# A decoder layer on one core: the steps that quantize the feed-forward's weights are spread over two batches instead of three

## The chip, the cores and the metric

The kernel runs on one core of a Trainium2 chip. The core has a matrix engine (TensorE; in the profile PE, with its weight loads as PEld), a vector engine (VectorE, DVE), an activation engine (ScalarE, ACT), a general engine (GpSimd, POOL) and SyncE (SP), which here only issues transfers. Sixteen DMA engines move data between the chip's main memory and the core's memories. Each engine works through its own queue in order; an instruction that waits holds up whatever is queued behind it on the same engine. The metric is device time in microseconds (us), the median of the runs; lower is better.

## The reference, cut to what matters

The kernel computes one decoder layer in float32 for a batch of four sequences of 512 rows of 512 numbers:

```python
x = x + attn(layernorm(x))                 # 16 heads over 128 x 128, all of a sequence's rows in q, k and v
x = x + gamma * xattn(layernorm(x), ctx)   # 8 heads, softmax over 512 keys
x = x + ffn(layernorm(x))

def ternary_quant(w):
    s = mean(abs(w))
    return clip(round(w / s), -1, 1) * s

def ffn(x):
    g = silu(x @ ternary_quant(w1).T) * (x @ ternary_quant(w3).T)
    return g @ ternary_quant(w2).T
```

w1 and w3 are 1365 x 512, w2 is 512 x 1365. A weight's scale s is a mean over the whole matrix, so quantizing takes two passes: one over all of it for the sum of absolute values, and one that compares each number with half the mean. The kernel keeps only the signs (-1, 0, 1), and applies s to the products.

## The kernel before, in words

**Stages.** The first batch's attention comes first (in the profile up to about 207 us). It loads the attention's weights, and keeps prepared copies of them (high parts, low parts and differences: `kept_kh`, `kept_kl`, `kept_kd` and so on) in main memory. Then a loop over b = 1, 2, 3 (line 989) does the attention of the second, third and fourth batch, about 216 us each. Within a batch a loop over j takes the four groups of heads. Each group makes three products, with the weights o (`values_out`, tiles `pu`), k (`keys_of`, `py`) and v (`values_of`, `pm`), and then the scores with q. A group's weights are 40 tiles of 256 KB, 12 each for o, k and v and 4 for q. They are loaded by SP (line 196) into a ring of 18 buffers (`wp`), so a load waits until an earlier tile's last matmul is done. At the end (from 858 us) all four batches go through the feed-forward.

**Work beside the products.** Two streams of small steps are woven between the products. Both are generators, and a class `Side` (line 165) advances them: after `done` calls of `tick()` out of `of`, it has taken `n * done / of` steps, rounded up. `products` (line 343) calls `tick` six times, so a batch has `TICKS` = 4 x 3 x 6 = 72 ticks.

- `side` is the cross-attention of the batch before (`cross`, line 694; tiles `xs`, `xp`, `xo`), after the row norms that it needs (`row_norms`). Its loads (`xd`, `kd`, `keys`, `xc`) and the store `x_c` are issued by POOL (line 703).
- `quant` is the quantizing of w1, w3 and w2, in this order (`quantize_steps`, line 621), 73 steps in all. w1 and w3 are cut into 12 pieces each, w2 into 11, of up to 128 x 512. A summing step takes a piece (`abs_w...`), and DVE sums its absolute values. After the last piece of a matrix, one step adds the sums up over the partitions (a matmul with one column) and makes the scales. A ternary step takes a piece again (`tern_w...`), DVE makes the signs (lines 652 and 653), and POOL stores them to main memory (`t_w...`, line 660).

**Loads of the pieces.** `staged` (line 595) issues them on POOL into a ring of three buffers, `stp`; `ahead` (line 612) issues a piece's load one step before the piece is used. A load into a buffer waits for what last used that buffer: DVE's sum of the piece before, or the landing of that piece's store.

**Order.** A planner orders each engine's queue when the kernel is built. It may bring an instruction forward when nothing that it needs is missing. The kernel therefore ties steps to a point in time by data: `settle` (line 606) multiplies a piece's first column by a one that DVE makes from `recent`, the latest product's tile (`one_of`, line 601). So DVE can't begin a piece before the product beside which the step stands. The loads into the staging buffers have no such tie. `tc.issue_after` puts some instructions behind another of their engine by name.

**Around it.** In the second batch (b = 1) DVE also makes difference tiles that the first batch did not keep (`od`, `kd`, `vd`, line 336), and POOL stores them. At the start of each batch POOL stores the attention's result (`x_a`), loads the next accumulators (`acc`) and adds the bias to them (line 872), and sends the row norms through main memory (`norm_a`, `norms`). At the end of the fourth batch SP loads the quantized weights (`t`, from 808 us on); the stores of w2 come last before that.

Of the kernel before, what the change touches and what calls it, by code (L numbers as in the profile page):

```python
# [20 lines left out]
B, T, D = 4, 512, 512  # L21
# [18 lines left out]
def decoder_layer_kernel(  # L40
# [124 lines left out]
    class Side:  # L165
# [5 lines left out]
        def tick(self):  # L171
            self.done += 1
            while self.n and self.n * self.done > self.of * self.taken:
                self.taken += 1
                next(self.steps, None)
# [249 lines left out]
    def parts_of(b, xs):  # L425
        tris = []
        for g in range(NG):
            tri = Tri(*(x3p.tile([P, D], F32R, tag="x3", name=f"x{p}_{b}_{g}") for p in "hld"))
            tri_of(tri, xs[g])
            tris.append(tri)  # L430
        return tris
# [4 lines left out]
    def gram_upper(b, xs, midway=None):  # L436
        pool, tag = (x3p, "x3") if b == 0 else (yp, "y")
        G = [pool.tile([P, D], F32, tag=tag, name=f"G_{b}_{m}") for m in range(KC)]
        pg = {}

        def add(m, g):
            if g == 0:
                pg[m] = bank(f"pg_{b}_{m}")
            nc.tensor.matmul(  # L444
                pg[m][:, : D - m * P],
                lhsT=xs[g][:, ts(m, P)],
                rhs=xs[g][:, m * P :],
                start=(g == 0),
                stop=(g == NG - 1),
            )  # L450
            if g == NG - 1:
                evict(G[m][:, m * P :], pg[m][:, : D - m * P])


        if b == 0:
            order = [(m, g) for g in range(NG) for m in range(KC)]
        else:
            order = [(m, g) for m in range(KC) for g in range(NG)]
        for m, g in order:
            add(m, g)  # L460
            if midway and (m, g) == (1, NG - 1):
                midway()
        return G

    def gram_rest(b, G):

        for rows in ((1, 2), (3,)):
            pt = bank(f"gt_{b}_{rows[0]}")
            n = 0
            for j in rows:  # L470
                for i in range(j):
                    nc.tensor.transpose(pt[:, ts(n + i, P)], G[i][:, ts(j, P)], ident)
                evict(G[j][:, : j * P], pt[:, n * P : (n + j) * P])
                n += j
        tris = []
        for m in range(KC):
            tri = Tri(*(g3p.tile([P, D], F32R, name=f"g{p}_{m}") for p in "hld"))
            tri_of(tri, G[m])
            tris.append(tri)
        return tris  # L480
# [73 lines left out]
    def turned(b, j, e):  # L554
        eT = ep.tile([P, NG, DH], F32, tag="eT", name=f"eT_{b}_{j}")
        transpose_blocks(eT, e, f"pe_{b}_{j}", True)
        return eT

    def output(b, j, eT, ms, accs):
        for g in range(NG):  # L560
            po = bank(f"po_{b}_{j}_{g}")
            nc.tensor.matmul(po, lhsT=eT[:, g, :], rhs=ms[g], start=True, stop=True)  # L562
            scale = (S if exact("o", b, j) else 1.0) * (S if exact("v", b, j) else 1.0)
            nc.vector.scalar_tensor_tensor(accs[g], po, scale, accs[g], ALU.mult, ALU.add)
            if j == HG - 1:
                nc.gpsimd.dma_start(by_group(x_a[b], g), accs[g])
# [54 lines left out]
    def quantize_steps(name):  # L621

        pieces = pieces_of(name)
        sums = small.tile([P, len(pieces)], F32, tag=f"sums_{name}", bufs=1, name=f"sums_{name}")
        nc.vector.memset(sums, 0.0)
        for piece, t, i in ahead(pieces, f"abs_{name}"):
            nc.vector.tensor_reduce(  # L630
                sums[: piece.shape[0], i : i + 1],
                piece,
                AX.X,
                ALU.add,
                apply_absolute_value=True,
            )
            yield
        col = small.tile([P, 1], F32, tag="col", name=f"col_{name}")
        nc.vector.reduce_sum(col, sums, axis=AX.X)
        tot = bank(f"tot_{name}")  # L640
        nc.tensor.matmul(tot[:, 0:1], lhsT=ones, rhs=col, start=True, stop=True)

        s = scales[name]
        for i, f in enumerate((0.5, -0.5, -1.0)):
            nc.vector.tensor_scalar(
                s[:, i : i + 1], tot[:, 0:1], 1.0 / (HID * D), f, ALU.mult, ALU.mult
            )
        yield
        for piece, t, i in ahead(pieces, f"tern_{name}"):
            r, n = piece.shape  # L650
            above = stp.tile([P, 512], BF16, tag="above", bufs=1, name=f"above_{name}_{i}")
            nc.vector.tensor_scalar(above[:r, :n], piece, s[:r, 0:1], None, ALU.is_gt)
            nc.vector.scalar_tensor_tensor(
                piece, piece, s[:r, 1:2], above[:r, :n], ALU.is_lt, ALU.subtract
            )
            for columns, place in t:
                part = piece[:, columns]
                if len(place.shape) > 2:
                    part = part.rearrange("p (u c) -> p u c", c=P)
                nc.gpsimd.dma_start(place, part)  # L660
            yield

    def quantize():
        for name in ("w1", "w3", "w2"):
            yield from quantize_steps(name)

    QUANTIZE_STEPS = 2 * (6 * KC + NHC) + 3
# [7 lines left out]
    def row_norms(b, accs):  # L675


        mv = small.tile([P, NG, 2], F32, tag="mvc", bufs=2, name=f"mv_c_{b}")
        for g in range(NG):
            yield  # L680
            yield
            moments(mv[:, g, :], accs[g], f"c_{b}_{g}")
        rstd = rstd_of(mv, f"c_{b}")
        mean, var = (mv[:, :, i : i + 1].rearrange("p c s -> p (c s)") for i in range(2))
        nc.vector.tensor_scalar(mean, mean, -1.0, None, ALU.mult)
        nc.vector.tensor_copy(var, rstd)
        nc.gpsimd.dma_start(norm_a[b].rearrange("(p g) s -> p g s", g=NG), mv)
        norms[b] = small.tile([P, 2 * NC, 2], F32, tag="norms", bufs=2, name=f"norms_{b}")
        for half in (slice(0, XD), slice(XD, P)):
            nc.gpsimd.dma_start(norms[b][half], norm_a[b].rearrange("(n p) s -> p n s", p=XD))  # L690
        for _ in range(3):
            yield
# [142 lines left out]
    TICKS = HG * 3 * 6  # L835
# [20 lines left out]
    def bias_rows(b):  # L856
        t = yp.tile([P, D], F32, tag="y", name=f"bo_bc_{b}")
        (nc.gpsimd if b > 0 else nc.sync).dma_start(t, bo.to_broadcast([P, D]))
        return t
# [21 lines left out]
    for j in range(HG):  # L881
# [19 lines left out]
        def midway():  # L901
            if waiting:
                waiting[2] = turned(*waiting[:3])
# [72 lines left out]
        inputs_f[b] = halves  # L976


    quant = Side(quantize(), QUANTIZE_STEPS, (B - 1) * TICKS)
    cpool = [  # L980
        cpools.enter_context(tc.tile_pool(name=n, bufs=k, side="right"))
        for n, k in (("c_x", 1), ("c_in", 2), ("c_p", 4), ("c_pt", 2))
# [6 lines left out]
    for b in range(1, B):  # L989
        def midway():  # L990
            waiting[2] = turned(*waiting[:3])

        G = gram_upper(b, xs, midway)
        recent[:] = [G[0], G[0]]
        output(*waiting)
        side = Side(
            itertools.chain(row_norms(b - 1, waiting[4]), cross(b - 1, *cpool)),
            NORM_STEPS + CROSS_STEPS,
            TICKS + 6,
        )  # L1000

        def tick():
            quant.tick()
            side.tick()

        bo_bc = bias_rows(b)
        g3 = gram_rest(b, G)
        for j in range(HG):
            u3 = values_out(b, j, x3, weights("o", b, j, wp), tick)
            if j > 0:  # L1010
                waiting[2] = turned(*waiting[:3])
            ys = keys_of(b, j, g3, weights("k", b, j, wp), tick)
            if j > 0:
                output(*waiting)
            else:
                accs = accumulators(b, bo_bc)
            if j == HG - 2:
                xs = rows_of(b + 1)
            if j == HG - 1 and b + 1 < B:
                normed(b + 1, xs, False)  # L1020
                x3 = parts_of(b + 1, xs)
            elif j == HG - 1:
                for t in xs:
                    settle(t)
                ffn_0 = prepare_ffn(0, xs)
                for _ in range(NC):
                    next(ffn_0)
            ms = values_of(b, j, weights("v", b, j, wp), u3, tick)
            e = scores(b, j, weights("q", b, j, wp), ys)
            waiting = [b, j, e, ms, accs]  # L1030
        side.rest()
# [155 lines left out]
```

## Time and profile before

| | us |
|---|---|
| median of 3 runs | 1158.3 (1157.48 to 1159.26) |
| the profiled execution | 1157.7, its span 1155.9 |
| PE busy in the span | 1144.6 (99%) |
| DVE busy | 818.9 (71%) |
| ACT busy | 524.5 (45%) |
| POOL busy | 318.8 (28%) |
| DMA, moved in the span | 270.16 MB, mean 234 GB/s |
| first and last sum of absolute values (L630) starts | 206.6 and 722.1 |
| first and last store of signs (L660) starts | 308.8 and 835.6 |
| first matmul of the feed-forward (L1094) starts | 858.8 |

A row of a group of instructions gives line, engine, operation, the tiles it writes and reads, how many there are, their busy time, and what ended the idle time before them. POOL's busy time counts its issues of transfers, half a microsecond or more each, but not the time in which it waits with one. Rows of windows give, for each stretch of the span, the busy time of each engine in us with the number of instructions, then the clock granted to PE, the mean busy share of the DMA engines (overlapping packets can take it over 1) and GB/s. In a row of waits stand the engine and line that waited, what it waited for, the us in total, the number of times and the longest. The chain of waits gives the start, the length and the work that the end of the kernel was waiting for at that time. A row of DMA issues gives the queue that issued, the number, the size and the median us from issue to landing.

### The profile page before, as it was taken

To read this page: it belongs to the slowest core of one execution; us is meant where nothing else is said; L and a number is where in the kernel's file an instruction comes from. 1 tells how busy PE (TensorE), PEld (TensorE's weight loads), DVE (VectorE), ACT (ScalarE), POOL (GpSimd) and SP (SyncE) were. 2 spreads that over 40 slices of the span, in tenths; PEclk is the share of its full clock that TensorE was granted. 3 is DMA by queue.
4 is the path that set the end of the run, shared out by engine and by line. 5 is a ranking of instruction groups with operands and counts; after the bars stand their busy time and mean duration, and the time that the engine had idled before them with its cause. 6 is when DMAs were issued, how large, how long until landed. Compare 5 with 4: busy or idle time off the path is not lost.

```text
span 1155.9 us, 16616 instructions
## 1 busy us (share of the span) xinstructions
PE 1144.6 (99%) x5282; PEld 856.5 (74%) x5282; DVE 818.9 (71%) x1802; ACT 524.5 (45%) x1073; POOL 318.8 (28%) x550
## 2 busy tenths in 40 slices
PE   8999999999999999999999999999999999999998
PEld 4486684777777768887786787777778877777886
DVE  6768657979797967869697758787957857536232
ACT  5434334435445443545354434544455768534020
POOL 3355443442232324112321332222112212000000
PEclk9999999999999999999999999999999999999999
DMA  9799996798889769997997699799881422122100
GB/s 327 251 329 322 343 359 231 248 331 279 260 292 332 232 235 323 298 286 249 325 305 253 211 345 295 226 336 320 295 282 58 128 82 64 46 74 73 64 1 37
DMA packets 145137, 270.16 MB, mean 234 GB/s; under 512 B 18252, under 2 KB 48260, under 8 KB 145050
## 3 DMA queue, kind: packets, MB, share of 16 engines
q1 hardware_dynamic: 111162, 164.40, 43.0%
q0 software_dynamic: 33872, 104.70, 26.8%
q8 instruction: 42, 0.69, 0.2%
q14 instruction: 45, 0.37, 0.1%
q10 hardware_dynamic: 16, 0.00, 0.0%
HBM read 206.10 MB, written 62.93 MB: 233 GB/s over the span
## 4 chain that ended last, share of the span: by engine, by line
PE 80%; DMA 2%; DVE 2%; issue 1%; ACT 0%; POOL 0%; DVEq 0%; ACTq 0%; POOLq 0%
PE h L1094 14%; PE y L1129 7%; PE xo L784 5%; PE xp L126 5%; PE po L562 4%; PE sc L523 3%; PE xs L740 2%; PE xs L741 2%; PE pg L444 2%; PE pu_1d L362 1%; PE pu_2h L350 1%; PE pm_2d L362 1%; PE pm_3h L350 1%; PE py_3h L350 1%; PE pm_3d L362 1%; PE pu_2h L351 1%
## 5 line engine op out<-in xcount | busy, mean ns | idle before, releaser
L1094 PE MATMUL h<-fxh,t 128*128 128x512 f32 (+1 forms) x352 | 139.6, 397 | 0.0
L1094 PE MATMUL h<-fxl,t 128*128 128x512 f32 (+1 forms) x352 | 137.4, 390 | 0.0
L751 ACT ACTIVATE p<-xs,xnmax 128x512 f32<-128x512 f32 x128 | 87.2, 689 | 82.9 <-PE xp L126 68.3
L745 DVE TENSOR_REDUCE xnmax<-xs 128x1 f32<-128x512 f32 x128 | 83.5, 684 | 23.9 <-PE xs L741 23.8
L1094 PEld LDWEIGHTS h<-fxh,t 128*128 128x128 f32 (+1 forms) x352 | 65.0, 185 | 15.4 <-issue 1.1
L1094 PEld LDWEIGHTS h<-fxl,t 128*128 128x128 f32 (+1 forms) x352 | 65.0, 185 | 14.7 <-issue 0.2
L1129 PE MATMUL y<-t,gh 128*128 128x512 f32 (+1 forms) x176 | 69.3, 394 | 0.0
L1129 PE MATMUL y<-t,gl 128*128 128x512 f32 (+1 forms) x176 | 68.8, 391 | 0.0
L129 ACT COPY pt<-xp 128x512 f32<-128x512 f32 x96 | 54.1, 595 | 30.7 <-PE xp L126 30.7
L126 PE MATMUL xp<-ident,p 128*128 128x128 f32 x512 | 66.5, 273 | 0.0
L126 PEld LDWEIGHTS xp<-ident,p 128*128 128x128 f32 x512 | 59.3, 140 | 9.4 <-issue 2.4
L703 POOL DMA_DIRECT2D xd<-x_a x64 | 33.8, 533 | 115.1 <-DVE qs L724 93.0
L784 PE MATMUL xo<-pt,vals 128*64 128x512 f32 x256 | 61.5, 599 | 0.0
L1107 DVE SCALAR_TENSOR_TENSOR gf<-h,scales_w,sl 128x512 f32<-128x512 f32 (+1 forms) x44 | 32.9, 747 | 39.7 <-PE h L1094 36.4
L763 DVE TENSOR_SCALAR p<-p,xrden 128x512 f32<-128x512 f32 x128 | 56.9, 487 | 3.0
L562 PE MATMUL po<-m,eT 128*128 128x512 f32 x128 | 58.1, 594 | 0.2 <-DVE y L372 0.2
L1103 ACT ACTIVATE sl<-h,scales_w 128x512 f32<-128x512 f32 (+1 forms) x44 | 30.1, 688 | 58.7 <-PE h L1094 58.5
L384 PE MATMUL pm<-u,v_raw 128*128 128x512 f32 x128 | 55.6, 592 | 0.0
L138 POOL CAST gh<-gf 128x512 fp32r<-128x512 f32 (+1 forms) x24 | 15.8, 660 | 137.2 <-DVE gf L1107 121.1
L740 PE MATMUL xs<-kh,qs 128*128 128x512 f32 x128 | 50.1, 392 | 0.0
L741 PE MATMUL xs<-kl,qs 128*128 128x512 f32 x128 | 50.0, 390 | 0.0
L139 DVE TENSOR_TENSOR gl<-gf,gh 128x512 fp32r<-128x512 f32 (+1 forms) x44 | 30.4, 690 | 25.6 <-POOL gh L138 18.6
(317 smaller groups left out, 2921.9 us busy)
## 6 DMA issues: line engine op xcount, KB each, us to landing
oh<-kept_oh SPq DMA_DIRECT2D x48, 256.0 KB, 6.4
ol<-kept_ol SPq DMA_DIRECT2D x48, 256.0 KB, 6.0
kh<-kept_kh SPq DMA_DIRECT2D x48, 256.0 KB, 5.9
kl<-kept_kl SPq DMA_DIRECT2D x48, 256.0 KB, 5.4
vh<-kept_vh SPq DMA_DIRECT2D x48, 256.0 KB, 6.8
vl<-kept_vl SPq DMA_DIRECT2D x48, 256.0 KB, 6.7
q<-kept_q SPq DMA_DIRECT2D x48, 256.0 KB, 6.3
od<-kept_od SPq DMA_DIRECT2D x44, 256.0 KB, 7.4
```

Source lines behind the costliest of these rows:

```text
L126: nc.tensor.transpose(pt[:, ts(k, P)], src[:, ts(k, P)], ident)
L129: nc.scalar.copy(dst, pv)
L384: nc.tensor.matmul(p, lhsT=lhs(k)[:, ts(i, P)], rhs=rhs(k), start=(k == 0), stop=(k == 3))
L562: nc.tensor.matmul(po, lhsT=eT[:, g, :], rhs=ms[g], start=True, stop=True)
L740: nc.tensor.matmul(sc, lhsT=q[:, ts(m, P)], rhs=kh, start=True, stop=False)
L741: nc.tensor.matmul(sc, lhsT=q[:, ts(m, P)], rhs=kl, start=False, stop=True)
L745: nc.vector.reduce_max(nmax[:, i : i + 1], scs[i], axis=AX.X)
L751: nc.scalar.activation(p, scs[i], AF.Exp, bias=nmax[:, i : i + 1], scale=xscale, accum_out=den[:, i : i + 1],)
L763: nc.vector.tensor_scalar(ps[i], ps[i], rden[:, i : i + 1], None, ALU.mult)
L784: nc.tensor.matmul(po[half, :], lhsT=vals[c][:, l, half], rhs=pt[j][:, l, :], start=(l == 0), stop=(l == NC - 1),)
L1094: nc.tensor.matmul(ph[:r, :], lhsT=t[:, block(i, k)], rhs=fxT[j][:, k, :], start=(k == 0 and j == 0), stop=(k == KC - 1 and j == 1),)
L1129: nc.tensor.matmul(py, lhsT=g[i][j][:r, ts(c, P)], rhs=t2[:r, i, :], start=(i == 0 and j == 0), stop=(i == NHC - 1 and j == 1),)
```

## The change

The quantizing takes no step beside the second batch (b = 1) any more. Its 73 steps are spread over the ticks of the third and fourth batch: 144 ticks instead of 216. The order of the steps, their work, their buffers and everything else stay as they are.

```diff
-    quant = Side(quantize(), QUANTIZE_STEPS, (B - 1) * TICKS)
+
+    quant = Side(quantize(), QUANTIZE_STEPS, (B - 2) * TICKS)
...
         def tick():
-            quant.tick()
+            if b > 1:
+                quant.tick()
             side.tick()
```

## The prediction

> **What bounds the kernel now.** The page comes first: it says which engine is full and whether its clock is.
>
> ```profile
> PE 1144.6 (99%) x5282; PEld 856.5 (74%) x5282; DVE 818.9 (71%) x1802; ACT 524.5 (45%) x1073; POOL 318.8 (28%) x550
> ...
> PEclk9999999999999999999999999999999999999999
> DMA  9799996798889769997997699799881422122100
> ```
>
> PE has work in 99% of the span, so an edit that leaves PE's work alone can win only the few us in which PE waits, and lose by making it wait. The other row that is full is DMA, until the feed-forward begins at 858 us. Next, busy time by batch (PE, PEld, DVE, ACT, POOL, clock, DMA share, GB/s; 207 to 424 is the second batch, then the third and fourth):
>
> ```profile
> 207.00:424.00 217.00, 216.08 (x1048) 164.07 (x1047) 182.66 (x426) 100.65 (x226) 72.34 (x120) 1.00 0.86 284
> 424.00:642.00 218.00, 217.95 (x1066) 167.06 (x1065) 167.86 (x398) 101.73 (x229) 58.57 (x98) 1.00 0.85 280
> 642.00:858.00 216.00, 216.00 (x1075) 167.42 (x1074) 166.13 (x387) 102.25 (x229) 53.36 (x92) 1.00 0.88 292
> ```
>
> DVE has 50 us free in the third and fourth, DMA 12 to 15% on average, unevenly, as windows of 5 us show:
>
> ```profile
> 655.00:660.00 5.00, 5.00 (x24) 4.14 (x23) 4.97 (x15) 3.70 (x6) 1.66 (x3) 1.00 0.81 246
> 660.00:665.00 5.00, 5.00 (x24) 3.99 (x22) 4.68 (x10) 2.34 (x4) 0.54 (x1) 1.00 1.01 386
> 685.00:690.00 5.00, 5.00 (x26) 4.21 (x26) 2.89 (x8) 3.40 (x11) 0.00 (x0) 1.00 1.04 345
> 740.00:745.00 5.00, 5.00 (x24) 2.49 (x24) 4.93 (x10) 2.50 (x5) 1.04 (x2) 1.00 0.30 97
> ```
>
> From 660 to 720 DMA is full. At the start of each batch the 18 weight buffers are still held, and the loads then have to catch up. The chain of waits in order of time shows that this is where PE is late now:
>
> ```profile
> 175.84 0.89 POOL abs_w L598 x2
> ...
> 180.01 5.78 DMA kept_vl<-v_l
> ...
> 234.54 4.08 DVE vd L336 x3
> ...
> 244.18 8.72 DMA oh<-kept_oh
> ...
> 461.40 9.87 DMA ol<-kept_ol
> ```
>
> Each is a place where PE waited: in the second batch for DVE's vd and for a load of o (j = 1), in the third for the same load by less, in the fourth not in the list. There the last od of j = 1 lands at 691.3 and the matmul that reads it starts at 691.4 (landing of the issue and start of its reader, of one trace): a cover of nothing. By the last vl of j = 1 (lands 711.2, read at 720.7) it is 9 us.
>
> **The change part by part.** There are 73 steps. Before, step s falls on tick 216(s-1)/73 + 1 (rounded down), one per 2.96 ticks; after, on 144(s-1)/73 + 1 counted from the third batch, one per 1.97. A batch of 218 us has 72 ticks, 3.0 us each: a step per 9.0 us becomes one per 6.0. A summing step is a 256 KB load (POOL issue 0.54) and on DVE 0.15 + 0.16 + 0.68 = 0.99 us; a ternary step a load, a store (POOL 0.72) and on DVE 0.15 + 0.16 + 0.48 + 0.75 = 1.54. ACT and SP get nothing; PE's three sums over partitions are one-column matmuls.
>
> DVE: some 24 steps, 12 of 0.99 and 11 of 1.54, leave the second batch (29 us), and half goes to each of the others: 168 + 15 = 183 us, what the second batch has now (182.7). Cover: its 35 us of rest, so 0; without that, as in the second batch, where the making of vd and kd came on top, under 1 us. The edit adds no wait; what a step's load waits for (its buffer), and what stands behind it on POOL, is the first rival.
>
> Second batch. From the first pu_0h to that of the next batch it takes 430.7 - 210.8 = 219.9 us, the third 648.7 - 430.7 = 218.0. The difference, 1.9, is vd behind DVE's queue and oh behind a full DMA. In 207 to 256, 6 loads of quantizing lie beside them (1.57 MB, 4.7 us at 333 GB/s) and 6 us of DVE. Without them: **-1.9**; ends -0.7 (vd's wait alone) and -2.6 (also what the third batch still waits).
>
> The three loads at 175.84. They are first read at 206.4 and wait for nothing but memory, in the first batch's last group. I expect them to be put there still, since the steps may go two hundred us later but their loads need no data: 0. If they are gone, kept_vl lands before DVE needs it, and what follows (PE idle 2.0 before the transposes of e at 201.96, then the clock's 0.83 and 0.82 over 10 us, 1.8 us of work) falls away: -3.8 at the other end.
>
> ```profile
> 200.00:205.00 5.00, 3.04 (x11) 2.49 (x12) 3.57 (x11) 3.43 (x12) 0.55 (x1) 0.83 0.01 3
> 205.00:210.00 5.00, 5.00 (x17) 3.15 (x16) 4.14 (x9) 0.64 (x2) 3.24 (x6) 0.82 0.71 243
> ```
>
> Third batch, first 22 ticks (430 to 475). Now 6 loads of w3; after, all 12 summing steps of w1, 9 loads with three ahead. 3 more, 0.79 MB at the 321 GB/s of this window, 2.4 us; shares of 0.76 to 0.91 up to 445 hide a part. **+1.0**; ends 0 and +2.4.
>
> Third batch, ticks 26 to 48. Now 4 summing and 3 ternary steps, 10 transfers; after, 12 ternary, 24: 14 x 0.23 MB, 10 us of DMA more in 70. The windows from 485 to 560 leave 13 us free, and weights have 4 to 9 us of cover. **+0.5**; ends 0 and +4.
>
> Fourth batch, first 25 ticks (648 to 697). Now one ternary step and 7 summing steps, which only read; after, the twelve ternary steps of w3, each with a load and a store. The DMA view of 655 to 691 has what is there now:
>
> ```profile
> DMA packets 6070, 11.99 MB, mean 333 GB/s; under 512 B 875, under 2 KB 875, under 8 KB 6067
> ...
> abs_w<-in_w2t_dram POOLq DMA_DIRECT2D x6, 256.0 KB, 5.6
> ...
> od<-kept_od SPq DMA_DIRECT2D x4, 256.0 KB, 8.6
> ```
>
> After, some 18 transfers of 0.23 MB (4.2 MB) instead of 1.6 MB: 2.6 MB, 7.9 us. Four fall before 660, where 4 us are free; the rest, 1.95 MB or 5.9 us, meets a full DMA and the od with no cover. **+5.0**, near the row's price since nothing else there waits; ends +2.3 (POOL gets only five pairs out) and +9 (all, with DVE behind it). While a weight is late, SP's queue behind it is too, but that is the same lateness.
>
> Fourth batch later. w2's ternary steps come every 6 us instead of 9, ticks 51 to 71. Weights have 7 to 8 us of cover, t_w's stores 5.3 each: **+0.5**; ends 0 and +3. The last step moves from tick 214 of 216 to 143 of 144, the last store from 835.6 to about 838; t2 behind it is first used past 900: 0.
>
> Sum: -1.9 + 0 + 1.0 + 0.5 + 5.0 + 0.5 = **+5.1 us**. The profiled execution took 1157.7 (span 1155.9 and 1.8 around it), 0.6 under the median of 1158.3. I put the sum on the median: **1163.4 us**.
>
> **The rivals.** *POOL becomes the bound.* The waits of the third batch:
>
> ```profile
> POOL tern_w L598 <- DMA t_w<-tern_w: 41.9, 8, 8.6
> ```
>
> POOL issues a store and then stands in the next load until that store has landed, with everything else of its queue behind (xd, kd, keys, acc). A ternary step holds it 0.72 + 5.3 + 0.54 = 6.6 us, and the cross-attention's fetches add 0.55: 7.1, within 9.0 now, over 6.0 after. 1.1 us per step is 13 over twelve; three buffers give 6.5 of lead; then DVE stands in line 610 for a piece, and all its evictions with it. 6.7 us a matrix, 20 for three, less where DVE's rest covers it: +12 in all, 1170.3. Against it: no DVE wait on tern_w now. It decides when a landing takes over 4.2 us. The Trainium skill, DMA: Bandwidth & Descriptors, section Anatomy of one DMA, speaks against it: about 2.0 us plus bytes at 436 GB/s, by which a 256 KB store would land in 2.6, hold POOL 4.4 and the rival would cost 0. The trace's median of 5.3 decides.
>
> *The loads at 175.84 leave (the other side).* Then -3.8 comes to -1.9. For: the steps are now programmed a batch later. Against: nothing holds a load that waits for no data. With +1.5 for the rest it gives 1154.1; it decides only if the fourth batch's loss stays under 3.4.
>
> *The weights keep their cover.* Stores may take less of DMA than loads, and POOL may spread the pairs. Then -1.9 + 1.0 + 1.0: 1158.4.
>
> *Nothing changes* can't be: 24 steps do move.
>
> **How the numbers follow.** A difference of 0.2% (2.3 us) is about what can be told from no change. Late weights (forecast) 0.5, of it 0.05 within the bound (own range 1160 to 1168); POOL 0.22; loads leave 0.15, of it 0.01 within; cover kept 0.13, of it 0.08 within, 0.04 slower, 0.01 faster. Faster 0.15, same 0.14, slower 0.71. The range leaves out the deeper half of the loads' case and POOL's last third: 1155.5 to 1175.
>
> **What would show it.** Right: the second batch's pu_0h to pu_0h falls to 218; PE's waits in 655 to 700 of the fourth batch on DMA od, kd, vd or ol, some 5 us; DMA 1.0 there. Wrong: the three abs_w loads no longer before 206; DVE idle on tern_w landings (POOL); DMA share under 1 in the fourth batch's first 45 us. What I may have misjudged is the order that the planner gives POOL, which the trace of before can't show.

## The result, and the profile after

| | median | runs |
|---|---|---|
| before | 1158.8 us | 1157.5 to 1160.8 |
| changed | 1195.4 us | 1191.9 to 1199.2 |

The changed kernel takes 1.0323 times as long (95% interval 1.0307 to 1.0338), some 36.6 us more. The profiled execution took 1194.0, with a span of 1192.3.

The page of the changed kernel, busy time first, then the granted clock and the DMA share in 40 slices:

```profile
PE 1154.3 (97%) x5282; PEld 858.3 (72%) x5282; DVE 817.3 (69%) x1802; ACT 524.8 (44%) x1073; POOL 316.7 (27%) x550
...
PEclk9999999999999999989999998999999999999999
DMA  9799995897686669987986697889974331121200
```

The same instructions ran on every engine, and VectorE was busy as long as before (817.3 against 818.9 us). PE is no longer full, and its clock sank in two slices. Busy time by batch (PE, PEld, DVE, ACT, POOL, clock, DMA share, GB/s):

```profile
207.00:424.00 217.00, 214.81 (x1049) 164.85 (x1048) 162.66 (x342) 101.06 (x227) 47.62 (x83) 1.00 0.75 246
424.00:642.00 218.00, 205.18 (x965) 157.02 (x964) 164.24 (x408) 93.45 (x207) 62.78 (x106) 0.97 0.85 274
642.00:890.00 248.00, 234.56 (x1150) 177.03 (x1150) 185.54 (x456) 107.27 (x246) 71.40 (x120) 0.99 0.86 288
```

From the first pu_0h to that of the next batch (the last: to the first h of the feed-forward), by the starts in the timeline:

| batch | before | changed |
|---|---|---|
| second | 219.9 | 220.2 |
| third | 218.1 | 237.9 |
| fourth | 210.1 | 228.2 |

The second batch, which the quantizing left, gained nothing. The third lost 19.8 us and the fourth 18.1. PE's waits, longest totals first, a few rows of the changed kernel (us in total, times, longest):

```profile
PE pu_2h L350 <- DVE m L372: 7.9, 1, 7.9
PE pu_1d L362 <- DVE m L372: 5.8, 1, 5.8
...
PE py_0d L362 <- DMA kd<-kept_kd: 2.4, 3, 1.2
PE pm_0d L362 <- DVE vd L336: 2.2, 2, 1.1
...
PE pm_0d L362 <- DMA vd<-kept_vd: 0.8, 1, 0.8
```

All rows together come to 33.6 us. In the kernel before they came to 7.1, nothing of it beside the third and fourth batch:

```profile
PE last_k L241 <- DMA k_last<-in_wk_dram: 3.6, 1, 3.6
PE pe L126 <- DVE e L549: 2.0, 1, 2.0
PE pm_0d L362 <- DVE vd L336: 0.7, 2, 0.5
```

Only 3.1 us of the 26.5 more are waits for transfers; the rest are waits for VectorE and ACT. What VectorE waited for in the changed kernel:

```profile
DVE tern_w L610 <- DMA tern_w<-in_w1t_dram: 14.5, 4, 10.4
...
DVE tern_w L610 <- DMA tern_w<-in_w3t_dram: 13.6, 5, 4.0
...
DVE abs_w L610 <- DMA abs_w<-in_w3t_dram: 8.8, 3, 5.3
...
DVE abs_w L610 <- DMA abs_w<-in_w2t_dram: 5.5, 1, 5.5
```

With the smaller rows this is 45 us of waiting for pieces, where the kernel before has no row of the kind. No row of VectorE waits for the cross-attention's fetches (xd, kd), although these stand behind the late loads on POOL. The chain of waits, in order of time, shows the two large holes:

```profile
513.03 7.52 DMA t_w<-tern_w
...
521.12 7.46 DMA tern_w<-in_w1t_dram
528.82 1.20 DVE xnmax L745 x2
530.85 0.69 DVE m L372
...
704.75 5.74 DMA t_w<-tern_w
711.08 5.40 DMA tern_w<-in_w3t_dram
717.68 1.28 DVE m L372 x2
```

A store lands, only then does the load of the next piece go out, and only when that has landed does VectorE get to the product (m) that PE needs. The timeline has the same place engine by engine (start, duration, what; in brackets the idle time before it and what ended it):

```profile
513.03 1.50 POOL L660 DMA_DIRECT2D t_w<-tern_w  x2
521.12 0.56 POOL L598 DMA_DIRECT2D tern_w<-in_w1t_dram  x1 [6.59 <-DMA t_w<-tern_w]
521.67 1.06 POOL L703 DMA_DIRECT2D xd<-x_a  x2
522.72 1.03 POOL L703 DMA_DIRECT2D kd<-in_kv_dram  x2
```

```profile
518.11 0.16 DVE L610 TENSOR_TENSOR tern_w<-tern_w,one 128x1 f32<-128x1 f32 x1 [0.89 <-DMA tern_w<-in_w1t_dram]
528.66 0.16 DVE L610 TENSOR_TENSOR tern_w<-tern_w,one 128x1 f32<-128x1 f32 x1 [10.38 <-DMA tern_w<-in_w1t_dram]
```

POOL stood 6.6 us before a load, the cross-attention's fetches (xd, kd) behind it, and VectorE 10.4 us. The two settles of VectorE belong to two steps that were let go by the same product; the second holds up the signs of the first piece as well, so its store left only at 531.2. The second part of the loss stands in windows of 5 us at the two holes, the long waits of PE:

```profile
520.00:525.00 5.00, 3.66 (x31) 3.23 (x29) 0.00 (x0) 0.00 (x0) 3.74 (x7) 1.00 1.05 381
525.00:530.00 5.00, 0.00 (x0) 0.00 (x0) 1.34 (x4) 0.00 (x0) 0.00 (x0) 0.75 1.06 272
530.00:535.00 5.00, 3.41 (x8) 2.74 (x9) 4.86 (x12) 2.41 (x6) 2.17 (x3) 0.50 0.66 233
...
713.00:718.00 5.00, 0.00 (x0) 0.00 (x0) 1.80 (x5) 0.00 (x0) 1.81 (x3) 0.72 0.93 271
```

The granted clock fell to 0.5 in the hole and stayed there after PE had work again. The trace has three such stretches in the batches (3.4 us from 449.0, 10.2 from 527.5, 6.8 from 715.2), 20.5 us at half speed, where before there was one of 3.4. In these 20.5 us PE was at work for 13.2 (3.4, 6.1 and 3.7); the rest lies inside the holes and is counted as waits already. Before, PE was at work in all of the 3.4. The work lost by the clock is then (13.2 - 3.4) / 2 = 4.9 us. Waits and clock together, 26.5 + 4.9 = 31.4, are most of the 36.4 us by which the span grew. The other 5.0 stand in PE's busy time, which grew by 9.7 us (1154.3 against 1144.6); no run here takes them apart.

### The profile page after: what moved, and what is told of

It reads as the page before. It is cut to its first block, busy times and chain, and to the rows that moved or that the text cites. A ratio compares the mean times of both kernels' runs of the same rounds, so it can differ in the third digit from the quotient of the medians.

```text
span 1192.3 us, 16632 instructions
## 1 busy us (share of the span) xinstructions
PE 1154.3 (97%) x5282; PEld 858.3 (72%) x5282; DVE 817.3 (69%) x1802; ACT 524.8 (44%) x1073; POOL 316.7 (27%) x550
## 4 chain that ended last, share of the span: by engine, by line
PE 45%; DMA 4%; issue 3%; DVE 3%; POOL 1%; ACT 0%; DVEq 0%; POOLq 0%; ACTq 0%
PE h L1096 13%; PE y L1131 7%; PE xo L784 3%; PE xp L126 3%; DMA t_w<-tern_w 2%; PE po L562 2%; PE xs L740 1%; PE xs L741 1%; PE sc L523 1%; DMA tern_w<-in_w3t_dram 1%; PE pu_2h L350 1%; PE pg L444 1%; PE pu_2h L351 1%; PE pm_3h L350 1%; DMA tern_w<-in_w1t_dram 1%
## 5 line engine op out<-in xcount | busy, mean ns | idle before, releaser
L1109 DVE SCALAR_TENSOR_TENSOR gf<-h,scales_w,sl 128x512 f32<-128x512 f32 (+1 forms) x44 | 32.9, 747 | 39.8 <-PE h L1096 36.4
```

## The experiments

Three notes on the quoted expectations: they count 75 steps where there are 73, and 28 stores where the trace has 43 (eight pieces are stored in two parts), and so their ticks per step (1.92, 2.40, 2.88 in place of 1.97, 2.47, 2.96) are a little small; e3's 2.88 is right.

**Is it the transfers, the stores, or VectorE's work?** Without the stores:

```diff
-                nc.gpsimd.dma_start(place, part)
...
-            load(t[:, c].bitcast(F32), kept_t[n][:, c])
+            raw = kept["k", 1 if n == "w1" else 2, "h"].rearrange("(p k) c -> p (k c)", k=KC)
+            load(t[:, c].bitcast(F32), raw[:, : c.stop - c.start])
...
```

> The changed kernel without the quantized pieces' 28 stores and their transfers (line 660); the feed-forward then reads other rows of the same sizes, so its output is left out as meaningless. The summing steps, the piece loads and every VectorE instruction of the 75 steps stay. Theory (the staging ring): in the changed kernel POOL's next piece load stands behind the landing of the last store (5 to 8 us), comes late, and VectorE waits for it at line 610 with the product evictions behind it. Without stores nothing on POOL waits for a landing, so the loads go out a step ahead: third batch 216 to 220 us instead of 237.9, fourth 209 to 214 instead of 228.2, in all 1156 to 1166. Rival (the 16 DMA engines are full and the weights come late, as forecast): 28 stores of some 256 KB are about 7 MB of the 120 MB that the two batches move, so a late weight gains perhaps a quarter of it: 1180 to 1190. Rival (VectorE has too much to do in a tick): no change, 1190 to 1198.

Measured 1166.8 us, 28.6 less than the changed kernel (ratio to before 1.0070, 1.0055 to 1.0085); third batch 223.7, fourth 217.2, VectorE's waits on pieces 7.9. The ring's number, just above its end. Then also without the piece loads:

```diff
-        piece = stp.tile([P, 512], F32, tag="stage", name=name)[:r, :n]
-        nc.gpsimd.dma_start(piece, src)
-        return piece
+        if "piece" not in mark:
+            mark["piece"] = stp.tile([P, 512], F32, tag="stage", name=name)
+            nc.gpsimd.dma_start(mark["piece"], w1t[0:P, 0:512])
+        return mark["piece"][:r, :n]
```

> As the kernel without stores, and also without the piece loads but one: every step works on the same tile in the staging pool, so sums and quantized values are left out as meaningless; VectorE's instructions of the 75 steps stay at their places, one step per 1.92 ticks of the third and fourth batch. Staging ring and full DMA engines alike: 1152 to 1160, with the third batch at 214 to 218 and the fourth at 208 to 211 (less than the kernel before had, as some 18 MB of transfers are gone). Rival (VectorE has too much to do): stays at 1180 to 1198. The difference to the kernel without stores is what the late landing of loads alone costs: 2 to 8 us.

Measured 1158.3 us, the kernel before's time (ratio 1.0005, 0.9989 to 1.0021), with the third batch at 218.6 and the fourth at 211.9. Its page:

```profile
PE 1143.1 (99%) x5282; PEld 855.8 (74%) x5282; DVE 815.3 (71%) x1802; ACT 524.4 (45%) x1073; POOL 251.1 (22%) x438
```

VectorE does the same 1802 instructions at the same density, and nothing is lost. VectorE's load is ruled out: the whole loss hangs on the pieces' transfers, with POOL's issuing of them and its waits (its busy time fell to 251.1 us). It also makes it likely that the kernel before loses little to these transfers: without any of them the time is at best 0.1% shorter than before (0.9989).

**Density or place?** Two matrices in the same two batches, and all three matrices in two other batches:

```diff
-        for name in ("w1", "w3", "w2"):
+        for name in ("w1", "w3"):
...
-    QUANTIZE_STEPS = 2 * (6 * KC + NHC) + 3
+    QUANTIZE_STEPS = 2 * 6 * KC + 2
...
```

> The changed kernel with only w1 and w3 quantized: 50 steps over the 144 ticks of the third and fourth batch, one per 2.88 ticks, as densely as the kernel before has them, but at the places of the changed one; the quantizing of w2 is left out, and the feed-forward reads other rows of the same size for it. Theory (density, through the ring: a step per 9 us leaves the store its 5 to 8 us of landing): 1155 to 1164, third batch 217 to 221, fourth 209 to 213. Rival (the place: these two batches have no room beside them, whatever the density): two thirds of the steps, two thirds of the loss, 1178 to 1188.

```diff
-            if b > 1:
+            if b < B - 1:
                 quant.tick()
```

> All 75 steps beside the second and third batch, one per 1.92 ticks as in the changed kernel, and none beside the fourth. Staging ring: the loss goes with the density: second batch 230 to 240 instead of 220, third 230 to 240 instead of 218, fourth 207 to 210, in all 1180 to 1200. Rival (full DMA engines, late weights): the share of the DMA engines is 0.85 in the second batch of the kernel before, against 0.89 in the fourth, so the loss falls to a third or less: 1160 to 1172. Rival (the place: the fourth batch, whose loss was 18 us): 1172 to 1180.

The sparser steps took 1162.0 us (1.0038, 1.0025 to 1.0051: 4 us more than before, not explained here), with no row of VectorE waiting for a piece's load; the dense steps elsewhere took 1193.7 us (1.0308, 1.0291 to 1.0325), with the second batch at 239.4, the third at 236.9 and the fourth at 209.5. So it is the density, wherever it is put. A dose between:

```diff
-    quant = Side(quantize(), QUANTIZE_STEPS, (B - 1) * TICKS)
+    quant = Side(quantize(), QUANTIZE_STEPS, 180)
...
-            quant.tick()
+            if b > 1 or j > 1:
+                quant.tick()
```

> A dose between the two kernels: the kernel before with its 75 steps beside the second half of the second batch, the third and the fourth: 180 ticks, one step per 2.40 ticks (7.3 us) instead of 2.88 (8.8) and 1.92 (5.9). Ring with pairs: two steps in one pair of products come in 18 of 60 pairs, with 14.6 us from one such pair to what follows, against 11 us of landings at the median and up to 17 at the slowest: a small part of the loss, 1160 to 1172. If the loss were in proportion to the density (36.6 us for 0.96 ticks less, so 18 for half of it): 1174 to 1180. If it has a threshold beyond this dose: 1157 to 1160.

Measured 1175.4 us (1171.5 to 1177.4; ratio 1.0150, 1.0120 to 1.0179). The ring with pairs had it too low, and proportion had it right; these three densities show no threshold.

**Which part of the ring?** A fourth buffer, its control with the weight buffer taken away alone, and a finer gate:

```diff
-        for n, k in (("a_w", 18), ("a_stage", 3))
+        for n, k in (("a_w", 17), ("a_stage", 4))
```

> The changed kernel with four staging buffers instead of three, paid for with one of the 18 weight buffers. All transfers and all VectorE instructions are as in the changed kernel. Theory (the ring: POOL stands at the next load because the buffer's last store has not landed): with four buffers the load needs the landing of a store that is one step older, so POOL hardly waits for a landing (58.6 us on tern_w loads and 31.5 us on abs_w loads in the changed kernel; below 20 together here) and the time falls near that of the kernel without stores (1166.8): 1163 to 1176, VectorE's waits on tern_w and abs_w loads below 12 us instead of 42. Rival (it is the stores' traffic that delays the loads, not the wait for their landing): 1188 to 1198.

> The control: the changed kernel with 17 weight buffers and still three staging buffers, so that the run with four can be read. Either theory: the weights come a little later, 1194 to 1203. If it is itself faster than the changed kernel by more than 5 us, the weight buffers are part of the story.

```diff
                 mark["copied"] = nc.scalar.copy(hs[i], ph[i]).ins
+            mark["gate"] = hs[pair[0]]
             tick()
...
         nc.vector.scalar_tensor_tensor(dst, h, 1.0 + 1.0 / S, d, ALU.mult, ALU.add)
+        mark["gate"] = dst
...
-                settle(here[0])
+                settle(here[0], mark["gate"])
```

> The changed kernel, in which the steps' gate (the value that a step reads, so that VectorE does not take it up too early; line 610's one) is renewed twice for a pair of products instead of once: when the half product has been copied and when the product is done. In the changed kernel two steps of one pair share a gate and follow each other on VectorE within 2 us (498.10 and 499.95, for instance), and then none comes for 7 us or more. Theory, sharper form (the ring fails because of the pairs: 12 us for two steps must hold a store's landing and a load's, 5.5 us each at the median, one after the other): spread steps leave each its own 6 us beside the other's transfers, 1163 to 1180. If the density alone does it, pairs or not: 1186 to 1198.

Four buffers: 1186.5 us (1.0249, 1.0226 to 1.0272); the control: 1199.5 (1.0363, 1.0333 to 1.0393); the finer gate: 1182.7 (1.0212, 1.0186 to 1.0238). The fourth buffer gains 13.0 us over its control, half of what was expected, and none of the two theories had its number. The finer gate gains 12.7, also between its two ranges: steps that come in pairs are a part, not the condition. POOL's waits, of the changed kernel and then with four buffers, say why the first theory, as I had put it, fell:

```profile
POOL tern_w L598 <- DMA t_w<-tern_w: 58.6, 16, 7.8
...
POOL abs_w L598 <- DMA t_w<-tern_w: 31.5, 6, 6.3
```

```profile
POOL tern_w L598 <- DMA t_w<-tern_w: 63.2, 18, 7.8
...
POOL abs_w L598 <- DMA t_w<-tern_w: 41.6, 7, 8.3
```

They have not shrunk below 20 us. POOL's timeline shows the order of its queue (three buffers, then four):

```profile
500.34 0.77 POOL L660 DMA_DIRECT2D t_w<-tern_w  x1 [0.59 <-DVE one L603]
508.05 0.54 POOL L598 DMA_DIRECT2D tern_w<-in_w1t_dram  x1 [6.95 <-DMA t_w<-tern_w]
508.58 1.28 POOL L660 DMA_DIRECT2D t_w<-tern_w  x2
```

```profile
503.00 0.77 POOL L660 DMA_DIRECT2D t_w<-tern_w  x1 [0.65 <-DVE one L603]
510.52 0.54 POOL L598 DMA_DIRECT2D tern_w<-in_w1t_dram  x1 [6.75 <-DMA t_w<-tern_w]
511.04 1.28 POOL L660 DMA_DIRECT2D t_w<-tern_w  x2
```

The load that takes over a buffer stands right behind the store that empties it, and ahead of the next store. It waits for that landing, and the next store waits in the queue behind it. Of the 22 such waits in the changed kernel, 16 are for the store just in front, with four buffers 17 of 25 (by the landings in the traces). Would the order alone do it, then?

```diff
-        nc.gpsimd.dma_start(piece, src)
+        behind = tc.issue_after(mark["stored"]) if "stored" in mark else ExitStack()
+        with behind:
+            nc.gpsimd.dma_start(piece, src)
...
-                nc.gpsimd.dma_start(place, part)
+                mark["stored"] = nc.gpsimd.dma_start(place, part).ins
```

> The changed kernel with four staging buffers and 17 weight buffers, as the run that came to 1186.5 us, but each piece load is tied behind the store that the program issued last, so that on POOL's queue it stands two stores behind the one that frees its buffer, not one. Buffers and transfers are those of that run. Theory (lockstep through the order on POOL): no load waits for a landing any more, and the time falls to about that of the kernel without stores: 1160 to 1172. Rival (the traffic, or too little lead for the loads): the loads now go out later than there, so 1186 to 1200.

> The same tie with three staging buffers and 18 weight buffers, as in the changed kernel. A load still needs the landing of a store, but of the last but one, which is a step (5.9 us) older at the nominal pace against a landing of 5.5 us at the median. Theory (lockstep through the order): 1163 to 1180. Rival: 1190 to 1200, as the changed kernel.

> The tied loads with four staging buffers, and the gate renewed twice for a pair of products. If order and pairs are all of the loss: 1156 to 1163, no more than 5 us above the kernel before (the third batch's late kd loads, some 3 us with the low clock behind them, stay). If the traffic has its own price, 1170 or more.

Measured 1198.5 us with four buffers (1.0355, 1.0338 to 1.0373), 1197.1 with three (1.0345, 1.0319 to 1.0370), 1193.5 with the finer gate (1.0310, 1.0287 to 1.0332). My sharper theory, lockstep through the order alone, fell. Waits of POOL, and of VectorE, in the run with four buffers:

```profile
POOL t_w L662 <- DVE tern_w L655: 85.2, 22, 12.0
```

```profile
DVE tern_w L612 <- DMA tern_w<-in_w3t_dram: 19.2, 6, 4.9
DVE tern_w L612 <- DMA tern_w<-in_w1t_dram: 12.7, 5, 4.8
```

In this run no load waits for a landing any more, but each stands behind a store that waits for VectorE. The load has no more time than in the changed kernel. My reading of this is that neither the landing nor the order counts for itself, but how long before its step a load gets out. The last group takes the landing out and leaves the load early. First with tiles of their own for the signs, two staging buffers and 17 of weights, and the same with three and 16:

```diff
+            signs = sgp.tile([P, 512], F32, tag="signs", name=f"signs_{name}_{i}")[:r, :n]
             nc.vector.scalar_tensor_tensor(
-                piece, piece, s[:r, 1:2], above[:r, :n], ALU.is_lt, ALU.subtract
+                signs, piece, s[:r, 1:2], above[:r, :n], ALU.is_lt, ALU.subtract
             )
...
-        for n, k in (("a_w", 18), ("a_stage", 3))
+        for n, k in (("a_w", 17), ("a_stage", 2), ("a_signs", 2))
```

> The changed kernel with the signs written to tiles of their own (two buffers), so that a staging buffer (two of them) is free for the next piece's load as soon as VectorE has read the piece, and POOL never waits at a load for a store's landing; one weight buffer of the 18 pays for it. All 43 store transfers and 70 piece loads stay, at the same ticks. Theory (a lockstep on POOL: the next load stands behind the landing of the store that POOL has just issued, so a ternary step costs a landing of 5.5 us and two issues of some 0.6 us each, 6.7 us where 5.9 us are to be had, whatever the number of buffers): near the kernel without stores (1166.8), 1163 to 1175. Rival (the stores' traffic, some 11 MB of transfers in engines that are 86% busy, as the forecast's late weights would have it): 1186 to 1200, as with four buffers (1186.5) or none more.

> The run with separate sign tiles (two), with three staging buffers instead of two; 16 weight buffers pay for it. No load waits for a store's landing, as in that run, but a piece has one buffer more to land in. If that run (1197.4) lost because two staging buffers give a load of 5.5 us too little lead: 1165 to 1180. If the traffic of the stores is the cause: 1190 to 1200 again.

Measured 1197.4 us (1.0336, 1.0309 to 1.0362) and 1183.1 us (1.0223, 1.0201 to 1.0245). The first is the rival's number, but not a clean test, since it takes a staging buffer away with the landing. The second lies between its two ranges. In it, VectorE's waits for pieces' loads are down to 2.2 us in the largest row (and 8.5 for a sign tile's last store), but TensorE waits 15.9 us for weights instead. Its PE waits on transfers, the largest but the first batch's:

```profile
PE pu_1h L351 <- DMA ol<-kept_ol: 4.8, 5, 1.8
...
PE pu_2h L351 <- DMA ol<-kept_ol: 2.5, 2, 1.8
PE pm_0h L351 <- DMA vl<-kept_vl: 2.3, 2, 2.0
```

So the same with signs of half the size, written over the comparison's tile, for one weight buffer:

```diff
-            above = stp.tile([P, 512], BF16, tag="above", bufs=1, name=f"above_{name}_{i}")
+            above = stp.tile([P, 512], BF16, tag="above", bufs=3, name=f"above_{name}_{i}")
...
+            signs = above[:r, :n]
             nc.vector.scalar_tensor_tensor(
-                piece, piece, s[:r, 1:2], above[:r, :n], ALU.is_lt, ALU.subtract
+                signs, piece, s[:r, 1:2], signs, ALU.is_lt, ALU.subtract
             )
...
-        for n, k in (("a_w", 18), ("a_stage", 3))
+        for n, k in (("a_w", 17), ("a_stage", 3))
```

> The changed kernel with the signs written in bfloat16 over the comparison's tile (three buffers of it instead of one), from where the stores take them and widen them; the staging buffer is free as soon as VectorE has read it. 17 weight buffers, three staging buffers, all 43 stores and 70 loads, the loads as early in POOL's queue as in the changed kernel. If the ring is the larger part of the loss, as the run without stores says (a gain of 28.6 us, of which the traffic is a part): 1166 to 1177, VectorE's waits on pieces below 5 us. If late weights are the larger part (stores' traffic in full DMA engines): 1180 to 1195, with waits of TensorE on weights of 10 us and more.

> As the run with bfloat16 signs, with the gate renewed twice for a pair of products. If ring and pairs are all there is besides the third batch's late kd loads: 1158 to 1166. If late weights remain: no better than without the second gate, within 4 us.

> The changed kernel without the stores, as the run that came to 1166.8 us, with 16 weight buffers instead of 18; its quantized weights are left out as there. If the run with separate sign tiles and 16 weight buffers (1183.1) lost by its fewer weight buffers: 1178 to 1184. If by the stores' traffic: 1165 to 1171.

Measured 1175.9 us (1.0153, 1.0136 to 1.0170), 1169.9 with the finer gate (1.0103, 1.0087 to 1.0118), and 1171.3 for the run without stores with 16 weight buffers (1.0121, 1.0101 to 1.0142). With all its transfers at the same ticks the kernel regains 23.5 us over its control (1199.5) when a landing no longer stands in front of the loads, and 29.6 with the gate. The first time is in its range, but VectorE still waits 15.1 us for pieces, not under 5; the second is 6.0 us better than without the gate and above the 1166 of ring and pairs alone, so it fits neither side. Two weight buffers fewer cost the run without stores 4.4 us, and TensorE waits 4.7 us for weights there. That is next to the range given for the stores' traffic: the late weights of the run of 1183.1 come from its stores beside few weight buffers, not from the few buffers alone. VectorE's waits on pieces in the run of 1169.9:

```profile
DVE tern_w L612 <- DMA tern_w<-in_w3t_dram: 6.2, 5, 2.6
...
DVE abs_w L612 <- DMA abs_w<-in_w1t_dram: 1.4, 1, 1.4
```

So the stores cost something beside the landing that loads wait for. The run of 1183.1 lies 11.8 us above its partner without stores (1171.3), VectorE's 8.5 us for the sign tiles included. The run of 1175.9 lies 9.1 above the one without stores and 18 weight buffers; one weight buffer less is perhaps 2 of it (an estimate, half of the 4.4). How the rest divides into traffic, POOL's time for the issues and landings that are slower there (6.1 us at the median) no run shows. The 12.4 us that remain over the kernel before are not settled in parts; 5.2 us of PE's waits in it are on late weights (kd, ol, od), which the kernel before does not have beyond 0.2.

One figure, worked out after these runs, sorts most of them into groups: the lead of a load, from when POOL's queue lets it go to when its step is due. At 9.0 or 6.0 us per step (7.5 in the dose) it is the number of steps between, less a landing of 5.5 us at the median where the load waits for one. The traces have it too: from the start of a ternary load's issue to VectorE's line 610 on its piece, the median over all ternary pieces.

| kernel | lead worked out, us | lead in the traces, us | time, us |
|---|---|---|---|
| before; two matrices | 3 x 9.0 - 5.5 = 21.5 | 21.7; 22.1 | 1158.8; 1162.0 |
| without stores; bfloat16 signs; separate signs, 16 weight buffers | 3 x 6.0 = 18.0 | 15.9; 14.4; 16.0 | 1166.8; 1175.9; 1183.1 |
| dose, 180 ticks | 3 x 7.5 - 5.5 = 17.0 | 16.6 | 1175.4 |
| changed | 3 x 6.0 - 5.5 = 12.5 | 12.6 | 1195.4 |
| tied loads with three and four staging buffers; two staging buffers | 2 x 6.0 = 12.0 | 7.3, 7.9; 8.2 | 1197.1, 1198.5; 1197.4 |

A load needs its landing (5.5 at the median and 9.3 at the most, loads and stores of ternary pieces together) and up to a step more when two steps share a gate. The four-buffer run (1186.5) should have 4 x 6.0 - 5.5 = 18.5, but its trace has 14.3: there the stores still stand behind waiting loads. The lead is not all. Within the second row the times differ by 16 us, and the changed kernel with the finer gate has 9.0 in its trace at 1182.7 us.

**The three loads at 175.84**, the other end of one term:

```diff
+        if name in ("abs_w1_0", "abs_w1_1", "abs_w1_2"):
+            nc.vector.tensor_copy(piece[:, 0:1], one_of(recent[-1])[:r, :])
         nc.gpsimd.dma_start(piece, src)
```

> The kernel before with its first three piece loads, which run at 175 us beside the end of the first batch, tied to the second batch's products, so that they run after 206 us. The forecast's other end said that their leaving 175 us would be worth up to 3.8 us (the wait of 2.0 us and the low clock at 203 us): 1154.4. The changed kernel kept the loads at 176 us and lost 2 us less in that place all the same, so the loads are not its cause: 1157 to 1159.

Measured 1162.1 us (1160.5 to 1164.7; ratio 1.0044, 1.0026 to 1.0061): worse, and outside what I expected. The low clock at 203 is gone, but the second batch now takes 227.8 us, with VectorE and the clock as the reason:

```profile
235.00:240.00 5.00, 2.35 (x11) 1.61 (x9) 5.00 (x3) 1.07 (x2) 4.98 (x6) 1.00 0.75 258
240.00:245.00 5.00, 3.48 (x8) 2.80 (x9) 4.85 (x9) 1.33 (x2) 3.88 (x7) 0.50 0.57 200
```

PE waits 4.2 us there for vd and 3.4 for kd, both made by VectorE. In this form at least, later loads are no gain.

## Why the prediction was wrong

The direction was right, but largely by luck: the mechanism of the forecast, late weights, came to 3.4 us of it. 1163.4 was forecast, in 1155.5 to 1175, and 1195.4 came. The step that failed is the one that put the quantizing's own pieces at nothing: the sum priced their transfers by free bandwidth and by the weights that they would make late, and left VectorE's wait for a late piece to a rival. In its place VectorE waited 45 us for pieces, and PE behind it 23.4 us more for VectorE and ACT, against 3.1 more for transfers. The terms, with the length of each stretch between the same products in both traces:

| stretch | forecast | measured |
|---|---|---|
| second batch | -1.9 | +0.3 |
| third batch, first 24 ticks (to py_1h) | +1.0 | +6.3 |
| third batch, ticks 25 to 48 (to pm_2h) | +0.5 | +11.6 |
| third batch, rest | 0 | +1.9 |
| fourth batch, first 24 ticks (to py_1h) | +5.0 | +13.1 |
| fourth batch, rest | +0.5 | +5.0 |

- **Fourth batch, first 25 ticks, +5.0 by late weights: failed, and here the most was lost.** PE waits 0.8 us for a weight (vd) in this stretch. The hole of 5.8 us at 712 lies in it, behind a ternary step of w3 whose load came late. The weights were not what the added transfers made late; the quantizing's own pieces were. Late weights as a whole cost PE 3.4 us (kd 2.4, vd 0.8, ol 0.2) against 0.2.
- **Third batch, ticks 26 to 48, +0.5: failed.** The term priced the transfers by their bandwidth, 10 us in 13 free. It left out that each has to fit into the time between its buffer's release and its step. The hole of 7.9 us at 523 and 10.2 us at half clock lie in this stretch.
- **Third batch, first 22 ticks, +1.0: right in kind, too small.** The kd loads came late by 2.4 us, the term's upper end, and 3.4 us at half clock followed. Without stores the 2.2 us of kd are there too; without piece loads they are gone.
- **Fourth batch later, +0.5.** w2's ternary steps, which the term was about, cost +0.3 (from pm_2h on). The +5.0 fell in ticks 25 to 36, where the sum had nothing; one wait of VectorE for a summing piece of w2, 5.5 us, lies there.
- **Second batch, -1.9: failed.** The prediction took pieces of the chain for waits of PE. PE's waits in the second batch of the kernel before were 0.9 us in all (vd 0.7, oh 0.2), so not 1.9 were to be won. In the changed kernel PE still waited 2.2 us for vd there, without any quantizing beside it, so quantizing was not what made vd late.
- **The loads at 175.84, 0: right**, they were issued at 176.6. Even so the low clock at 203 is not in that trace, so the loads alone do not make it. The term's other end had the wrong sign in the one form tried: tying them to later products cost 4.9 us.
- **VectorE, 0: right.** The run without transfers does all of VectorE's work at this density in the time of before.
- **The first rival, POOL's wait for the landing, had the mechanism and 0.22 of the chance.** Store, landing, load, then VectorE in line 610 with its evictions (its copies of PE's products) behind: every link is in the chain above, and the 26 stores of 256 KB in the changed kernel's DMA view took 5.5 us to land at the median, on the rival's side of its 4.2:

```profile
t_w<-tern_w POOLq DMA_DIRECT2D x26, 256.0 KB, 5.5
```

Its sign, VectorE idle on tern_w, came as well. (The 5.3 us of the prediction mix the stores with SP's later loads of the same tile; the 256 KB stores alone took 5.2 before. Both are over 4.2.) The rival's price of 12 was too low in three terms: VectorE waited 45 us for pieces, not 20; steps in pairs, which it did not count, are worth 12.7 us by the run with the finer gate; and the half clock behind the holes 4.9. I gave the rival less than half the forecast's chance since the trace of before had no such wait of VectorE. That argument was empty: before, POOL's own wait for landings was larger than after, and harmless.

```profile
POOL tern_w L598 <- DMA t_w<-tern_w: 114.5, 24, 8.6
```

This row is of the kernel before; the changed one has 58.6. A wait off the path says nothing of the slack it uses; the lead has to be worked out.

The figure that the Trainium skill gives for such a transfer (DMA: Bandwidth & Descriptors, Anatomy of one DMA: about 2.0 us plus the bytes at 436 GB/s, 2.6 us for a 256 KB store) spoke against this rival. The measured median of 5.5 us, in DMA engines that were busy 85% of the time and more in the third and fourth batch, decides against it; what makes up the difference of 2.9 us no run here takes apart.

## What to carry to other kernels

For work that is slipped in beside a full engine, don't price its transfers by free bandwidth alone: work out the lead of each load (buffers times the time per step, less every landing that its queue makes it wait for) and compare it with the slow landings of the trace, not the median. When steps are packed closer this lead shrinks by more than the time per step, as the landing stays: here a third less time per step took the lead from 21.5 to 12.5 us. A helper engine that processes its queue in order turns a late side transfer into a late product. Look at which instruction stands in front of the load in its queue before adding buffers: a buffer more, or another order, helps only if the load really gets out earlier.

## What the hardware showed

The clock fell to 0.5 in and behind PE's holes, and the time at half speed came in pieces of 3.4, 6.8 and 10.2 us, all multiples of 3.41; after the hole of 7.9 us it began 3.8 us into the hole and lasted 6.1 us into the work. Three waits for kd in 444 to 448, 2.4 us together, were enough for 3.4 us of it. The lengths, the half rate and the late start are as the Trainium skill has it (TensorE: Matmul & The Clock Gate, What's actually happening: half the rate after one idle window of about 3.4 us, full again after a busy one, the windows running freely). But the window before need not be idle throughout: in the 3.41 us ahead of the three falls PE was at work for 1.46 (at 449.0), 0 (527.5) and 0.80 us (715.2), and for 1.36 ahead of the fall in the kernel before (203.3). After windows with 2.94 and 2.22 us of work (from 442.2 and 708.4) the clock stayed full. I had priced holes by their length alone; here the clock added 4.9 us of lost work to 26.5 us of waits.
